# Moving the coefficient and artanh chains of layer 1 from VectorE to GpSimd in a four-layer graph network

## The chip, the cores and the metric

The kernel runs on one core of a Trainium2 chip. Its time is the device time of the core in microseconds, the median of several runs; lower is better. The engines are TensorE (PE), VectorE (DVE), ScalarE (ACT), GpSimd (POOL) and SyncE (SP), each with its own queue of instructions that it works through in order. Every DMA is issued from SyncE.

## The reference

128 graphs of 64 nodes with 128 features, and a sparse weighted adjacency matrix per graph, pass four layers. Each layer is a residual: `x = x + layer(relu(layernorm(x)), adj)`. The change touches layer 1, a graph network in hyperbolic space, and the small bias of layer 0 in front of it. Cut to what matters here (c = 1):

```python
y = ssp(y @ Wd1.T + bd1) @ Wd2.T + bd2          # end of layer 0
...
h = proj(mobius_add(proj(mobius_matvec(W, x)), hyp_bias))        # "nodes"
x_loc = logmap(h_i, h_j)                                          # for all pairs
a = silu(concat(x_self, x_loc) @ att_w1.T + att_b1)               # "edges"
adj_att = sigmoid(a @ att_w2.T + att_b2)
support = sum_j(adj_att * x_loc * mask)
u = silu(concat(x_self, support) @ mlp_w1.T + mlp_b1) @ mlp_w2.T + mlp_b2 + x_self
second = tanh(0.5 * lambda_x(h) * norm(u)) * u / norm(u)
out = proj(mobius_add(h, second))                                 # "rest1"
xt = silu(artanh(norm(out)) * out / norm(out))
out = proj(tanh(norm(xt)) * xt / norm(xt))
```

`mobius_add(x, y)` is `(ca * x + cc * y)`, with the coefficients `ca = (1 + 2xy + y2) / den`, `cc = (1 - x2) / den`, `den = 1 + 2xy + x2*y2` of three scalar products per node. All this is per node: one number per row of 128 features, so four numbers per partition in the layout below.

## The kernel before

**Tiling.** Eight graphs form a group: four pairs of graphs, a pair on the 128 partitions (64 nodes each). There are 16 groups. A tile of node features is 128x4x128 (128x512), a tile of pairs of nodes 128x4x64 (128x256), and a number per node is a 128x4 tile. Edges are packed into slots (512 columns for most, 264 for the last block), so edge tiles have 1024 or 528 columns.

**Stages of a group.** load; order (nodes sorted by degree; its side stream normed_x makes sr, a and xp, the last two with 128x512 products on GpSimd); layer0 (a filter per edge); layer1_nodes (end of layer 0, h, then the coefficients pq, qn and Sx of the edges); layer1_edges (attention scores, ex and th on ScalarE); rest1 (the sum over the neighbours, u, the Mobius addition, artanh, silu); rest2 (layers 2 and 3). The stages of neighbouring groups overlap: while edges and rest1 of groups g and g-1 run, order, layer0 and nodes of later groups do too.

**What sets the order.** Each stage is a Python generator that says, by `yield on(engine, ...)`, on which engine its next piece runs. A planner (class Weave) picks the pieces one by one: earliest possible start by its own costs, then a key that is the stage's rank plus a number from the table LATE for each piece. So the order of each engine's queue is fixed when the program is built, and every engine keeps it even where a piece turns out late. The planner counts four engines, their latencies and the rings of buffers. Its costs on GpSimd, for n columns, are one line:

```python
    return (0.5 + 0.14 * n) if ALU.pow in args else 0.18 + 0.0024 * n
```

**ScalarE's tables.** exp and ln need one table, silu and tanh another. The main loop runs the pieces in stretches of one table, and leaves a stretch only when named events have come: the silu stretch ends when the edges of a group and the silu part of rest1 (`rest1_silu`) of the group before are issued.

**The parts that change.** `layer1_nodes` begins by adding the bias bd1 to a PSUM tile on DVE. At its end it splits pq into three bf16 parts (pqs) and Sx into three (S3), all differences on DVE. `rest1` computes u, its norm un2 (ScalarE, sums of squares), then `un` by a power on GpSimd; `rb`, `ur`, `k_` and the coefficients d_ca, d_cc (function `mobius`) on DVE with four columns each; ScalarE scales hh by d_ca, DVE adds cc times u; ScalarE sums the squares again (d_n2), GpSimd takes the root (d_hn), DVE runs `artanh_over` to get the factor d_r, and ScalarE applies silu with the scale d_r. After that comes one more norm (un, ur, k_) and x2.

GpSimd has a power function: `power(dst, src, e)` is a tensor_tensor with ALU.pow against a constant tile, so it also serves as reciprocal and square root.

Of the kernel before, what the change touches and what calls it, by code (L numbers as in the profile page):

```python
# [29 lines left out]
MAXNORM = 1.0 - 0.004  # L30
# [741 lines left out]
PE, DVE, ACT, POOL = "PE", "DVE", "ACT", "POOL"  # L772
# [12 lines left out]
def about(engine, op, args, kw):  # L785
# [14 lines left out]
    if engine == ACT:  # L800
# [5 lines left out]


LATE = {
    "attention": (0, -0.5),
    "coefs_of": (1.25, 0.75, -2.25),  # L810
    "coefs_of2": (2.75,),
    "duo": (2.5, 3.5),
    "duo2": (0, 2.5, -2),
    "filter_of": (0.75, 3, -0.25, -2.25, -2, -2.75),
    "filter_of2": (-2.75, 1.75, 2.5, 1.75, -2.5),
    "layer1_nodes": (0, -0.25, 0, 0, 0, 0, 0, 3, -3.5, 0, 0, 0, -0.5, -5.5, 0, 2.25, -1.75, 0, 0, 0,
        0, 0, 0, -2.5, 0, 0, 0, 0, 0, -1.25, 0, 0, 0, 2, 0, 0.75, 0, 0, 0, 0, 0, 0, 0, 0, 0.5),
    "neighbours": (-0.25, -3.5),
    "neighbours2": (1.25,),
    "normed_x": (0, 0, 0, 0, 0, 0, 1.5),  # L820
    "one_minus_z": (3.75,),
    "order": (-0.25, -2.75, 2.25, 0, 0, -5, 0, -3.75, 0, 1.75, -6.75, -3, 3.5, 0, 0, -2.75, -2.75,
        3.25, 1.75, 0.5),
    "rest1": (-3, 0, 0, -3, 0, 0, 0, -3.5, -1.75, 0, 0, 0, 0, 0, -1.75, 0, 0, 0, 3.75),
    "rest2": (2.25, 4.5, 0, 0, 0, 0, 0, 0, 0, 0, 0, -4, 0, -3.75, 0, 1.25, 0, 0, 0, 0, -3, 0, -2.25,
        0, -3.5, 0, 0, 1.25, 3),
    "rows": (0, -1.25),
    "rows2": (2.5,),
    "scores_of": (-1.25, -1.5, -3.5, -1.5),
    "scores_of2": (0, -3.25, 0, -3.5),  # L830
    "slots_ranks": (3.5, 0, 4.75),
    "squares": (2.25, 9.5),
    "squares2": (0, 2.75),
    "turned_from": (3.5,),
    "weights_of": (-3,),
    "weights_of2": (0, -2.5, -2.25),
}


# [30 lines left out]
def on(engine, *takes, after=(), table=None):  # L870

    return engine, takes, after, table
# [98 lines left out]
def sparse_stack(ctx: ExitStack, tc: tile.TileContext, ins, out: bass.AP, flag):  # L971
# [7 lines left out]
    dense = ctx.enter_context(tc.tile_pool(name="s_dense", bufs=1))  # L979
# [106 lines left out]
    b1, bd1, b2s = (column("L0_gnn_" + n) for n in ("b1", "bd1", "b2"))  # L1086
# [49 lines left out]
    hby2 = const.tile([P, 1], F32, name="hby2")  # L1136
# [101 lines left out]
    act = S.activation  # L1238
# [43 lines left out]
    def power(dst, src, e):  # L1282

        G.tensor_tensor(dst, src, exps[e][:, 0:elements(src)], ALU.pow)
# [38 lines left out]
        act(dst, src, AF.Ln)  # L1323
        act(dst, dst, AF.Exp, scale=e)

    def artanh_over(r, s, hn):


        E, ef, num, den, q = (ttile(f"ah{k}") for k in range(5))
# [6 lines left out]
        V.scalar_tensor_tensor(num, E, 1.0, s, ALU.add, ALU.mult)  # L1336
        V.tensor_scalar(q, E, -1.0, 1.0, ALU.mult, ALU.add)
        V.tensor_tensor(num, num, q, ALU.add)
        V.tensor_tensor(den, q, s, ALU.mult)
        V.scalar_tensor_tensor(den, den, 1.0, E, ALU.add, ALU.add)  # L1340
        V.reciprocal(den, den)
        V.tensor_tensor(num, num, den, ALU.mult)
        V.tensor_tensor(den, num, num, ALU.mult)
        V.tensor_scalar(q, den, 1.0 / 9, None, ALU.mult)
        for c in (1.0 / 7, 1.0 / 5, 1.0 / 3):
            V.scalar_tensor_tensor(q, q, c, den, ALU.add, ALU.mult)
        V.scalar_tensor_tensor(q, q, 1.0, num, ALU.add, ALU.mult)
        V.tensor_tensor(q, q, ef, ALU.add)
        V.reciprocal(den, hn)
        V.tensor_tensor(r, q, den, ALU.mult)  # L1350

    def part(t, at, k, n):

# [284 lines left out]
        w.event("layer0", g)  # L1638


    def mobius(ca, cc, xx, xy, y2):

        den = ttile("den")
        V.tensor_scalar(ca, xy, 2.0, 1.0, ALU.mult, ALU.add)
        V.tensor_tensor(den, xx, y2, ALU.mult)
        V.tensor_tensor(den, den, ca, ALU.add)
        V.tensor_tensor(ca, ca, y2, ALU.add)
        V.tensor_scalar(den, den, 1e-15, None, ALU.max)
        V.reciprocal(den, den)
        V.tensor_tensor(ca, ca, den, ALU.mult)  # L1650
        V.tensor_scalar(cc, xx, -1.0, 1.0, ALU.mult, ALU.add)
        V.tensor_tensor(cc, cc, den, ALU.mult)

    def layer1_nodes(g, st):

# [3 lines left out]
        spn, ex = wtile("a0"), wtile("a1")  # L1659
        pt = bank()  # L1660
        pre = flat(pt)
# [73 lines left out]
        s, r = ttile("s"), ttile("r")  # L1735
# [6 lines left out]
        z, rs, mask = ttile("at_z"), ttile("at_r"), ttile("at_k")  # L1742
# [34 lines left out]
        mobius(ca, cc, xx, xy, hby2.to_broadcast([P, NP]))  # L1777
        V.tensor_tensor(ca, ca, t, ALU.mult)
        yield on(ACT)
        for p in range(NP):  # L1780
# [3 lines left out]
        hn, sc = ttile("hn"), ttile("sc")  # L1784
# [110 lines left out]
        cs = ttile("cs", bufs=2)  # L1895
        reduce_d(cs, dc)

        yield on(DVE, after=[("U", g)])
        pqs = dense.tile([P, 3, NP, N], BF, name="pqs", tag="pqs")
        V.tensor_copy(pqs[:, 0], pq)  # L1900
        V.tensor_tensor(e4, pq, pqs[:, 0], ALU.subtract)
        V.tensor_copy(pqs[:, 1], e4)
        V.tensor_tensor(pqs[:, 2], e4, pqs[:, 1], ALU.subtract)
# [99 lines left out]
    def rest1(g, st):  # L2003
# [53 lines left out]
        def product_with_h():  # L2057
            yield on(POOL)
            G.tensor_tensor(tmp2, u, hh, ALU.mult)
            yield on(DVE)  # L2060
            reduce_d(uh, tmp2)
            V.tensor_scalar(rb, st["beta"], 1e-15, None, ALU.max)
            V.reciprocal(rb, rb)
# [16 lines left out]
        V.tensor_tensor(xy, uh, k_, ALU.mult)  # L2080
        V.tensor_tensor(un2, un2, k_, ALU.mult)
        V.tensor_tensor(un2, un2, k_, ALU.mult)
# [9 lines left out]
        squares_sum(hn2, tmp, u)  # L2092
        yield on(POOL)
        G.tensor_scalar(hn2, hn2, MIN_NORM2, None, ALU.max)
        power(hn, hn2, 0.5)
# [7 lines left out]
        squares_sum(un2, tmp, u)  # L2103
        yield on(POOL)
        G.tensor_scalar(un, un2, MIN_NORM2, None, ALU.max)
        power(un, un, 0.5)
# [4 lines left out]
        V.reciprocal(ur, un)  # L2111
# [191 lines left out]
```

## Time and profile before

| | |
|---|---|
| time, median of 3 runs | 2124.41 us (2123.33 to 2126.65) |
| the profiled execution: its time, its span | 2121.52 us, 2119.6 us |
| granted TensorE clock, mean | 0.94 |
| VectorE, TensorE, ScalarE, GpSimd busy | 1847.9, 1806.3, 1641.1, 364.5 us |
| instructions on VectorE, ScalarE, GpSimd | 4828, 3364, 362 |
| DMA | 13.94 MB, 7 GB/s on the mean |

The span is the time from the first to the last instruction. A busy time is the union of an engine's instructions, without register, branch, semaphore and DMA-issuing ones. Nearly all instructions are recorded by one helper (line 853), so that groups have to be told apart by the tiles they write and read (`out<-in`), not by line. In a group's row stand the count, the total busy time and the mean of one; in a tile's row the smallest, middle and largest duration in ns. In the timeline the columns are start, duration, engine, operation, tiles and shapes.

Between the start (about 240 us) and the tail (from about 1860 us) the program repeats group by group. There VectorE is busy 1516.0 of 1620 us and TensorE 1450.6; in the tail, where less is left to overlap, VectorE is busy 161.8 of 259.6 us.

### The profile page before, as it was taken

The page shows a single profiled execution, that of the slowest core. Times are in us where ns is not written, and L with a number is a line of the kernel's source. Part 1 is how long each engine was busy: PE and PEld are TensorE (multiplying, and loading weights), DVE is VectorE, ACT ScalarE, POOL GpSimd, SP SyncE. Part 2 cuts the span into 40 slices and gives each one's busy share as a digit, 9 for nine tenths or more (in the row PEclk, how much of TensorE's full clock was granted, in tenths as well). Part 3 has the DMA queues.
Part 4 walks back from the last instruction along what each step waited for, and adds up shares of the span by engine and source line. Part 5 has one row for each costly group of instructions (what it writes and reads, how often), then busy time and mean ns, then how long its engine had stood idle before and what let it go on. Part 6 is the DMA issues. An engine that isn't in the chain of part 4 may idle for free.

```text
span 2119.6 us, 31941 instructions
## 1 busy us (share of the span) xinstructions
PE 1806.3 (85%) x11223; PEld 866.0 (41%) x11223; DVE 1847.9 (87%) x4828; ACT 1641.1 (77%) x3364; POOL 364.5 (17%) x362
## 2 busy tenths in 40 slices
PE   4869897998989898998989889898989889896773
PEld 2333343444444344444444444444434444443342
DVE  5669789999999999999999999999999999897742
ACT  3767887979698887979798897969888796975531
POOL 1011012021212203021221202121220302111121
PEclk9979999999999999999999999999999999997765
DMA  2000000000000000000000000000000000000000
GB/s 55 3 6 1 1 6 1 6 8 6 1 8 6 8 6 8 6 8 6 1 8 6 9 6 9 6 1 8 6 9 1 9 1 6 1 1 6 6 5 8
DMA packets 29531, 13.94 MB, mean 7 GB/s; under 512 B 10544, under 2 KB 29360, under 8 KB 29360
## 3 DMA queue, kind: packets, MB, share of 16 engines
q1 hardware_dynamic: 29360, 11.80, 2.1%
q8 instruction: 90, 1.47, 0.3%
q14 instruction: 81, 0.66, 0.1%
HBM read 7.61 MB, written 4.19 MB: 6 GB/s over the span
## 4 chain that ended last, share of the span: by engine, by line
PE 37%; DVE 36%; ACT 19%; issue 7%; POOL 0%; SPq 0%; DMA 0%; DVEq 0%; ACTq 0%; POOLq 0%
PE big L853 25%; PE sm L853 9%; ACT ex L853 6%; DVE va L853 5%; DVE ex L853 4%; PE sl L853 4%; ACT e L853 4%; DVE th L853 4%; DVE y L853 2%; ACT ra L853 2%; DVE ah L853 2%; DVE v L853 2%; ACT n L853 2%; DVE att L853 2%; DVE oh L853 1%
## 5 line engine op out<-in xcount | busy, mean ns | idle before, releaser
L853 PE MATMUL big<-ex,w2T 128*128 128x512 f32 (+1 forms) x768 | 320.2, 542 | 41.8 <-ACT ex L853 20.6
L853 ACT ACTIVATE ex<-big,c_L_gnn_att_b 128x1024 f32<-128x1024 f32 (+1 forms) x192 | 185.5, 974 | 105.0 <-PE big L853 103.2
L853 PE MATMUL big<-e,w1T 64*128 64x512 f32 (+1 forms) x768 | 201.5, 624 | 68.0 <-ACT e L853 47.8
L853 ACT ACTIVATE ex<-big,c_L_gnn_b 128x1024 f32<-128x1024 f32 (+1 forms) x192 | 185.7, 976 | 44.1 <-PE big L853 44.0
L853 PEld LDWEIGHTS big<-ex,w2T 128*128 128x128 f32 x768 | 131.7, 189 | 198.6 <-ACT ex L853 69.5
L853 PE MATMUL big<-va,U 64*128 64x512 f32 (+1 forms) x768 | 186.5, 563 | 29.1 <-DVE va L853 26.8
L853 PE MATMUL big<-va,a 64*128 64x512 f32 (+1 forms) x768 | 181.1, 568 | 10.7 <-DVE k_s L853 3.8
L853 PE MATMUL sl<-ex,aw2b 128*64 128x512 f32 (+1 forms) x768 | 180.7, 549 | 5.5 <-ACT th L853 4.3
L853 DVE SCALAR_TENSOR_TENSOR ex<-big,c_L_gnn_b,ra 128x1024 f32<-128x1024 f32 x128 | 163.7, 1279 | 16.0 <-PE big L853 15.6
L853 ACT ACTIVATE ex<-ex 128x1024 f32<-128x1024 f32 (+1 forms) x192 | 173.9, 925 | 0.2
L853 ACT ACTIVATE ra<-big 128x528 f32<-128x528 f32 (+1 forms) x192 | 166.3, 886 | 8.1 <-PE big L853 7.6
L853 DVE TENSOR_REDUCE y<-ex 128x128 f32<-128x1024 f32 x128 | 155.3, 1213 | 0.6
L853 ACT ACTIVATE th<-sl,hab 128x512 f32<-128x512 f32 (+1 forms) x192 | 118.1, 615 | 45.4 <-PE sl L853 45.4
L853 PE MATMUL big<-slot_r,Sx 64*128 64x512 bf16 (+1 forms) x1152 | 138.9, 346 | 0.0
L853 POOL TENSOR_TENSOR k_r<-k_r,exp 128x4 f32<-128x4 f32 x32 | 32.4, 1013 | 583.1 <-DVE k_r L853 578.7
L853 PEld LDWEIGHTS big<-e,w1T 64*128 64x128 f32 x768 | 68.9, 204 | 155.6 <-ACT e L853 55.1
L853 ACT ACTIVATE va<-va,sr 128x512 f32<-128x512 f32 (+1 forms) x192 | 123.1, 650 | 3.1 <-DVE va L853 2.9
L853 PE MATMUL big<-oh,pqs 64*64 64x512 bf16 (+1 forms) x1152 | 123.3, 348 | 0.0
L853 DVE COPY_PREDICATED va<-slot_r,big 128x1024 f32<-128x1024 uint16 (+1 forms) x96 | 106.5, 1111 | 9.7 <-PE big L853 9.7
L853 DVE SCALAR_TENSOR_TENSOR th<-th,oh 128x1024 f32<-128x1024 f32 (+1 forms) x80 | 99.2, 1240 | 13.8 <-ACT th L853 13.8
L853 ACT ACTIVATE e<-e 128x1024 f32<-128x1024 f32 (+2 forms) x144 | 106.7, 752 | 1.1
L853 PE MATMUL big<-va,ones 64*64 64x512 f32 (+1 forms) x768 | 97.4, 559 | 11.0 <-DVE va L853 11.0
(479 smaller groups left out, 3832.4 us busy)
## 6 DMA issues: line engine op xcount, KB each, us to landing
x<-in_x_dram SPq DMA_DIRECT2D x16, 256.0 KB, 2.9
out_dram<-v SPq DMA_DIRECT2D x16, 256.0 KB, 2.3
adj<-in_adj_dram SPq DMA_DIRECT2D x16, 128.0 KB, 2.3
rt<-in_L_gnn_att_w_dram SPq DMA_DIRECT2D x2, 64.0 KB, 1.9
rs<-in_L_gnn_mlp_w_dram SPq DMA_DIRECT2D x2, 64.0 KB, 2.0
wupd<-in_L_gnn_W_upd_dram SPq DMA_DIRECT2D x1, 128.0 KB, 3.6
w<-in_L_gnn_W_msg_dram SPq DMA_DIRECT2D x2, 64.0 KB, 3.3
r_L_gnn_bd<-in_L_gnn_bd_dram SPq DMA_DIRECT2D x1, 64.0 KB, 3.1
```

What stands on the lines that cost most here:

```text
L853: return f(*args, **kw)
```

## The change

Six edits and a new order:

1. bd1 is added by ScalarE (Identity with a bias) instead of DVE.
2. The first two bf16 parts of pq are made by ScalarE; the two differences stay on DVE.
3. The two differences of the split of Sx move from DVE to GpSimd, between ScalarE's two copies.
4. In rest1 everything from `rb` to `cc * k_` moves from DVE to GpSimd, reciprocals as powers with exponent -1; `mobius` takes the engine as an argument (the call in layer1_nodes keeps DVE).
5. `artanh_over` becomes `artanh_parts` (five operations on DVE) and `artanh_of` (18 operations and a power on GpSimd), with the division by the norm as a power of -0.5 and a product after it. The bound of s moves to GpSimd.
6. `ur` is a power of -0.5 on GpSimd, placed in front of the power that makes `un`, in both norms.

The table LATE has other numbers throughout, which changes the order of the pieces on every engine.

```diff
 LATE = {
-    "attention": (0, -0.5),
-    "coefs_of": (1.25, 0.75, -2.25),
...
+    "attention": (0, 0, 3.5, 1),
+    "duo": (4.5, 6.5),
...
-    for e in (0.5, -0.5, -0.25):
+    for e in (0.5, -0.5, -0.25, -1.0):
...
+    def artanh_of(r, E, ef, s):
+
+        num, den, q, z = (ttile(f"ah{k}") for k in range(2, 6))
+        G.tensor_scalar(num, E, 1.0, None, ALU.add)
+        G.tensor_tensor(num, num, s, ALU.mult)
+        G.tensor_scalar(q, E, -1.0, 1.0, ALU.mult, ALU.add)
+        G.tensor_tensor(num, num, q, ALU.add)
+        G.tensor_tensor(den, q, s, ALU.mult)
+        G.tensor_scalar(z, E, 1.0, None, ALU.add)
+        G.tensor_tensor(den, den, z, ALU.add)
+        power(den, den, -1.0)
+        G.tensor_tensor(num, num, den, ALU.mult)
+        G.tensor_tensor(z, num, num, ALU.mult)
+        G.tensor_scalar(q, z, 1.0 / 9, 1.0 / 7, ALU.mult, ALU.add)
+        for c in (1.0 / 5, 1.0 / 3, 1.0):
+            G.tensor_tensor(q, q, z, ALU.mult)
+            G.tensor_scalar(q, q, c, None, ALU.add)
+        G.tensor_tensor(q, q, num, ALU.mult)
+        G.tensor_tensor(r, q, ef, ALU.add)
...
-    def mobius(ca, cc, xx, xy, y2):
+    def mobius(E, ca, cc, xx, xy, y2):
...
-        V.reciprocal(den, den)
...
+        (power(den, den, -1.0) if E is G else V.reciprocal(den, den))
...
-        yield on(DVE)
-        V.tensor_scalar(flat(spn), pre, bd1, None, ALU.add)
-        w.release("sm")
+        yield on(ACT)
+        act(flat(spn), pre, AF.Identity, bias=bd1)
+        w.release("sm")
+        yield on(DVE)
...
+        for k in range(2):
+            yield on(ACT)
+            act(pqs[:, k], (pq, e4)[k], AF.Copy)
+            yield on(DVE)
+            V.tensor_tensor((e4, pqs[:, 2])[k], (pq, e4)[k], pqs[:, k], ALU.subtract)
...
-            yield on(DVE)
-            V.tensor_tensor(Sx if k == 0 else S3[2], Sx, S3[k], ALU.subtract)
+            yield on(POOL)
+            G.tensor_tensor(Sx if k == 0 else S3[2], Sx, S3[k], ALU.subtract)
...
         yield on(POOL)
+        G.tensor_scalar(rb, st["beta"], 1e-15, None, ALU.max)
+        power(rb, rb, -1.0)
         G.tensor_scalar(un, un2, MIN_NORM2, None, ALU.max)
+        power(ur, un, -0.5)
         power(un, un, 0.5)
-        yield on(DVE, after=[("uh", g)])
-        V.tensor_tensor(rb, rb, un, ALU.mult)
-        V.reciprocal(ur, un)
+        G.tensor_tensor(rb, rb, un, ALU.mult)
         yield on(ACT, table="silu")
         act(k_, rb, AF.Tanh)
-        yield on(DVE)
-        V.tensor_tensor(k_, k_, ur, ALU.mult)
+        yield on(POOL, after=[("uh", g)])
+        G.tensor_tensor(k_, k_, ur, ALU.mult)
         xy, ca, cc = ttile("d_xy"), ttile("d_ca"), ttile("d_cc")
...
-        mobius(ca, cc, h2, xy, un2)
-        V.tensor_tensor(cc, cc, k_, ALU.mult)
+        mobius(G, ca, cc, h2, xy, un2)
+        G.tensor_tensor(cc, cc, k_, ALU.mult)
...
         power(hn, hn2, 0.5)
-        yield on(DVE)
-        V.tensor_scalar(s, hn, MAXNORM, None, ALU.min)
-        artanh_over(r, s, hn)
+        G.tensor_scalar(s, hn, MAXNORM, None, ALU.min)
+        yield on(DVE)
+        artanh_parts(E, ef, s)
+        yield on(POOL)
+        artanh_of(r, E, ef, s)
+        power(hn2, hn2, -0.5)
+        G.tensor_tensor(r, r, hn2, ALU.mult)
```

More of the change, by code (lines that the diff above doesn't have):

```diff
@@ L808 @@
 LATE = {
-    "attention": (0, -0.5),
-    "coefs_of": (1.25, 0.75, -2.25),
[L811 to L819, printed above, removed]
@@ L820 @@
-    "normed_x": (0, 0, 0, 0, 0, 0, 1.5),
-    "one_minus_z": (3.75,),
[L822 to L834, printed above, removed]
+    "attention": (0, 0, 3.5, 1),
+    "duo": (4.5, 6.5),
+    "duo2": (1.25,),
+    "filter_of": (1.5, 3.5, -1.75, 0, 0, -1.5),
+    "filter_of2": (-2.5, 1.5, 2.5, 4),
+    "layer1_edges": (0, 0, 0, -4),
+    "layer1_nodes": (0, 0, 0, 0, 0, -3.5, 0, 0, -2.75, 0, 0, 3, 2.25, 0, 3.5, 3.75, 0, -3.5, 0, 0,
+        0, 0, 3, 0, 0, 0, 0, 0, 0, 0, 0, 2.25, 2.5, 2.5, 0, 0, 0, 2.75, 0, 0, 0, 0, 0, 0, 0, 1.5, 0,
+        0, 0, -3.25),
@@ new lines @@
+    "neighbours": (0, -2.25),
+    "neighbours2": (0, 2.25),
+    "norm_of_h": (4.25,),
+    "normed_x": (2.75,),
+    "one_minus_z": (3.75,),
+    "order": (0, 0, 0, 1.5, 0, -2.75, 0, 0, 0, 5.5, -1.5, 0, 0, 0, 0, 2.5, 0, 0, 2, -4),
+    "product_with_bias": (0, 3.25),
+    "rest1": (-3, 0, -3.25, -3.25, 0, 0, 0, -3.5, 0, -3.25, 0, 0, 0, 0, 0, 1.75, 0, -1.5),
+    "rest2": (0.25, 0, 0, -3.5, 0, 0, 0, 0, 1.25, 0, 0, 0, 0, 0, 0, 1.75, 0, 0, -2.25, 0, -3, 0, 0,
+        0, 0.75, -1.75, -4, 0, 2.25),
@@ L835 @@
+    "rows": (-1, -3.5),
+    "rows2": (1.75,),
+    "scores_of": (-1.25, 0, -2.5),
+    "scores_of2": (0, 0, 0, -5),
+    "slots_ranks": (2.25,),
+    "squares": (2.25, 7.5),
+    "turned_from": (0, 4),
     "weights_of": (-3,),
-    "weights_of2": (0, -2.5, -2.25),
+    "weights_of2": (0, 0, -0.75),
 }
@@ L1324, in root, with artanh_parts @@
         act(dst, dst, AF.Exp, scale=e)
-    def artanh_over(r, s, hn):
-        E, ef, num, den, q = (ttile(f"ah{k}") for k in range(5))
+    def artanh_parts(E, ef, s):
         V.tensor_scalar(E, s, -ROOT_HALF, ROOT_HALF, ALU.mult, ALU.add)
@@ L1335, in artanh_over @@
                         ALU.add, ALU.mult)
[L1336 to L1340, printed above, removed]
-        V.reciprocal(den, den)
[L1342 to L1350, printed above, removed]
+    def artanh_of(r, E, ef, s):
[16 more added lines that the diff above has]
+        G.tensor_tensor(r, q, ef, ALU.add)
     def part(t, at, k, n):
@@ L1638, in layer0 @@
         w.event("layer0", g)
-    def mobius(ca, cc, xx, xy, y2):
[L1643 to L1652, printed above, removed]
+    def mobius(E, ca, cc, xx, xy, y2):
+        den = ttile("den" if E is V else "g_den")
+        E.tensor_scalar(ca, xy, 2.0, 1.0, ALU.mult, ALU.add)
+        E.tensor_tensor(den, xx, y2, ALU.mult)
+        E.tensor_tensor(den, den, ca, ALU.add)
+        E.tensor_tensor(ca, ca, y2, ALU.add)
+        E.tensor_scalar(den, den, 1e-15, None, ALU.max)
+        (power(den, den, -1.0) if E is G else V.reciprocal(den, den))
+        E.tensor_tensor(ca, ca, den, ALU.mult)
+        E.tensor_scalar(cc, xx, -1.0, 1.0, ALU.mult, ALU.add)
+        E.tensor_tensor(cc, cc, den, ALU.mult)
     def layer1_nodes(g, st):
@@ L1776, in layer1_nodes @@
         V.tensor_tensor(xx, xx, t, ALU.mult)
-        mobius(ca, cc, xx, xy, hby2.to_broadcast([P, NP]))
+        mobius(V, ca, cc, xx, xy, hby2.to_broadcast([P, NP]))
         V.tensor_tensor(ca, ca, t, ALU.mult)
@@ L1896, in layer1_nodes @@
         reduce_d(cs, dc)
-        yield on(DVE, after=[("U", g)])
[L1899 to L1903, printed above, removed]
-        yield on(DVE)
+        pqs = dense.tile([P, 3, NP, N], BF, name="pqs", tag="pqs")
+        for k in range(2):
[3 more added lines that the diff above has]
+            V.tensor_tensor((e4, pqs[:, 2])[k], (pq, e4)[k], pqs[:, k], ALU.subtract)
+        yield on(DVE, after=[("U", g)])
         Sx, S3 = st["Sx"], [wide.tile([P, NP, P], BF, name=f"Sx{k}", tag=f"Sx{k}") for k in range(3)]
@@ L2061, in product_with_h @@
             reduce_d(uh, tmp2)
-            V.tensor_scalar(rb, st["beta"], 1e-15, None, ALU.max)
-            V.reciprocal(rb, rb)
             w.event("uh", g)
@@ L2069, in rest1 @@
         yield on(POOL)
+        G.tensor_scalar(rb, st["beta"], 1e-15, None, ALU.max)
+        power(rb, rb, -1.0)
         G.tensor_scalar(un, un2, MIN_NORM2, None, ALU.max)
+        power(ur, un, -0.5)
         power(un, un, 0.5)
-        yield on(DVE, after=[("uh", g)])
-        V.tensor_tensor(rb, rb, un, ALU.mult)
-        V.reciprocal(ur, un)
+        G.tensor_tensor(rb, rb, un, ALU.mult)
         yield on(ACT, table="silu")
         act(k_, rb, AF.Tanh)
-        yield on(DVE)
-        V.tensor_tensor(k_, k_, ur, ALU.mult)
+        yield on(POOL, after=[("uh", g)])
+        G.tensor_tensor(k_, k_, ur, ALU.mult)
         xy, ca, cc = ttile("d_xy"), ttile("d_ca"), ttile("d_cc")
-        V.tensor_tensor(xy, uh, k_, ALU.mult)
-        V.tensor_tensor(un2, un2, k_, ALU.mult)
-        V.tensor_tensor(un2, un2, k_, ALU.mult)
-        mobius(ca, cc, h2, xy, un2)
-        V.tensor_tensor(cc, cc, k_, ALU.mult)
+        G.tensor_tensor(xy, uh, k_, ALU.mult)
+        G.tensor_tensor(un2, un2, k_, ALU.mult)
+        G.tensor_tensor(un2, un2, k_, ALU.mult)
+        mobius(G, ca, cc, h2, xy, un2)
+        G.tensor_tensor(cc, cc, k_, ALU.mult)
         yield on(ACT)
@@ L2094, in rest1 @@
         G.tensor_scalar(hn2, hn2, MIN_NORM2, None, ALU.max)
+        E, ef = ttile("ah0"), ttile("ah1")
         power(hn, hn2, 0.5)
+        G.tensor_scalar(s, hn, MAXNORM, None, ALU.min)
         yield on(DVE)
-        V.tensor_scalar(s, hn, MAXNORM, None, ALU.min)
-        artanh_over(r, s, hn)
+        artanh_parts(E, ef, s)
[3 more added lines that the diff above has]
+        G.tensor_tensor(r, r, hn2, ALU.mult)
         yield on(ACT, table="silu")
@@ L2105, in rest1 @@
         G.tensor_scalar(un, un2, MIN_NORM2, None, ALU.max)
+        power(ur, un, -0.5)
         power(un, un, 0.5)
@@ L2110, in rest1 @@
         yield on(DVE, "x2")
-        V.reciprocal(ur, un)
         V.tensor_scalar(k_, k_, MAXNORM, None, ALU.min)
```

## The prediction

> **What bounds the kernel now.** First the page's busy times: VectorE (DVE) leads, TensorE (PE) is next, GpSimd (POOL) is nearly free.
>
> ```profile
> PE 1806.3 (85%) x11223; PEld 866.0 (41%) x11223; DVE 1847.9 (87%) x4828; ACT 1641.1 (77%) x3364; POOL 364.5 (17%) x362
> ```
>
> The chain's shares say that no engine holds the end alone.
>
> ```profile
> PE 37%; DVE 36%; ACT 19%; issue 7%; POOL 0%; SPq 0%; DMA 0%; DVEq 0%; ACTq 0%; POOLq 0%
> ```
>
> In its middle the program repeats every 121 us, once per group. ScalarE (ACT) splits a period by its table loads; the timeline gives the edges (two more loads, inside the silu stretch, serve the softplus).
>
> ```profile
> 1148.18 1.28 ACT L853 ACT_TABLE_LOAD   x1
> 1206.83 1.28 ACT L853 ACT_TABLE_LOAD   x1
> 1269.02 1.28 ACT L853 ACT_TABLE_LOAD   x1
> ```
>
> So 58.65 us with silu tables, 62.2 us with log tables, 120.8 together. Busy time in the two:
>
> ```profile
> core 0: us, PE busy (x) PEld busy (x) DVE busy (x) ACT busy (x) POOL busy (x), PEclk, DMA share, GB/s
> 1148.20:1206.80 58.60, 54.12 (x372) 25.80 (x371) 56.92 (x131) 43.93 (x101) 15.10 (x14) 1.00 0.03 8
> 1206.80:1269.40 62.60, 54.66 (x330) 26.19 (x331) 57.60 (x169) 58.67 (x111) 7.81 (x8) 0.97 0.02 5
> ```
>
> In the silu stretch DVE is busy 97%, PE 92%, ACT 75%; in the log stretch ACT leads with 94%. DVE work is worth time in the first only, ACT work is dear in the second.
>
> The silu stretch carries rest1, one long dependent chain: u, the coefficients k_, d_ca, d_cc, the update of w, its norm, the artanh chain to d_r, then ACT's silu with d_r. In the timeline u is ready at 1155.15 and ACT begins with d_r at 1184.09: **28.9 us**.
>
> **What the Trainium skill says.** "SBUF — State Buffer", section "Who interferes with whom": DVE and GpSimd share one port pair under an exclusive lock. A DVE instruction with two SBUF inputs and a GpSimd instruction that reads SBUF exclude each other; one with a single SBUF input does not contend. The trace agrees:
>
> ```profile
> 1038.81 2.52 POOL L853 TENSOR_TENSOR a<-xp,o_mv 128x512 f32<-128x512 f32 x1
> 1040.35 1.00 DVE L853 TENSOR_TENSOR rb<-rb,un 128x4 f32<-128x4 f32 x1
> 1041.37 2.25 DVE L853 TENSOR_TENSOR oh<-pos,slot_k 128x2048 bf16<-128x2048 bf16 x1
> 1041.42 3.33 POOL L853 TENSOR_TENSOR xp<-xp,r_L_gnn_bd 128x512 f32<-128x512 f32 x1
> 1043.54 1.22 DVE L853 TENSOR_TENSOR k__9670<-k__9670,ur 128x4 f32<-128x4 f32 x1
> ```
>
> The xp product alone takes 1.27 us; here it waits out the 2.25 us oh instruction, and then the four-column k_ product waits 1.06 us for it. Four-column GpSimd operations get stuck too:
>
> ```profile
> L853 POOL TENSOR_SCALAR un<-un x32: 227/232/1160, 307.1 to 2072.1; 128x4 f32<-128x4 f32 x32
> L853 POOL TENSOR_TENSOR d_hn<-d_n,exp x16: 1037/1312/4315, 320.6 to 2064.5; 128x4 f32<-128x4 f32 x16
> ```
>
> The 4.3 us one sat behind th (1.21) and oh (2.28) in a row. In the other direction they cost DVE nothing visible: beside a power at 1074.3 four x updates ran in 1.14 us, as elsewhere. "GPSIMD Engine Reference", section "Elementwise — side-by-side cycle accounting", has GpSimd's tensor_tensor at 1.96 times DVE's; here 128x512 take 1.27 against 0.68 us, 1.9 times.
>
> **The change part by part**, per group. The order of instructions shows what each engine issues: DVE loses 656, 41 a group; GpSimd gains 43; ACT 3; PE, SyncE, DMAs and table loads keep their numbers.
>
> - *DVE.* Artanh 16 instructions 2.61 us (0.15 to 0.18 each) and the s bound 0.16; rb 1.13 (three), ur 0.33 (two), k_ by ur 1.22; xy, un2 twice and cc by k_ 0.64; mobius 9 for 1.48; bd1 0.74; two casts 0.58; two Sx differences 1.37. Sum 10.3 us. Of this 1.9 (0.84 at rb, 1.06 at k_) is waiting for a and xp, which stay and will hold other two-input instructions. Real relief: **8.4 us**, 6.5 in the silu stretch, 1.9 in the log stretch.
> - *ACT.* bd1 as an Identity from PSUM, 0.60 (nearest row: a<-sm, 596 ns), and two 128x256 copies, about 0.41 each: +1.4 us. The order also moves ACT work. At start-to-start steps of dense stretches (1.00 us for 1024 columns, 0.60 for 528, 0.56 for 512, 0.36 for 256, 0.32 for 128) the log stretch holds 58.6 us before and 62.2 after, the silu stretch 38.5 and 36.2. Where 58.6 took 62.2 us, 62.2 take **66.0**.
> - *GpSimd.* 35 four-column operations, start to start 0.31 (1156.66 to 1156.97); 6 powers, 1.1; two 128x512 differences, 1.27: 10.9 + 6.6 + 2.5 = 20 us on top of 22.9. No throughput limit. The two differences may hold DVE up to 1.27 us each; beside the one-input reductions and PSUM reads of the log stretch I take half, and offset it with that stretch's DVE relief. Sx has about 15 us of DVE work until the scores need it, so its slower chain costs nothing.
>
> **The rest1 path** decides. From u, on free ports: u by hh to 1.4; rb pair to 2.8; un, two powers (the new ur one stands first) and rb by un to 5.6; tanh 5.95; ten small operations and a power, ca at 10.1; cc at 11.0; w update 12.1. On GpSimd sr, its power, a and xp now stand between d_cc and d_n: 3.9 us, to 14.9. d_n, power, s to 16.6; five DVE instructions to 17.6; 18 small and one power to 24.3; last power and product: d_r at **25.7**, better than 28.9.
>
> With the lock it is later. Followed with DVE's new order beside it (va spreads 1.2 us, th 1.2, oh pieces 0.3 to 0.4, v+x 0.7: two SBUF inputs each), one GpSimd operation passes per such DVE instruction instead of three or four. cc comes at 15 to 16, so DVE, whose own work before the w update lasts 10.5, waits 4 to 5 us. sr, a and xp push d_n to 20 or 21; artanh takes 9 or 10 instead of 8.1: d_r at 31.5 to 34. The bounds are 25.7 and 34; I take **30.5**: nearer the contended end, because instructions with two SBUF inputs fill half of DVE's silu stretch today (29 of 58.6 us, added up from the timeline), and below it, because a waiting DVE frees the port.
>
> While d_r is late, ACT stands before the silu with d_r; behind it in ACT's queue are softplus, the th and ex of the scores, hence PE's PSUM banks. That is the new wait.
>
> Period: log 66.0; silu load to u 4.6 (load 1.3, v copy and hid 1.2, PE 1.3, u 0.7, where before v's four pieces and a ra stood there too); u to d_r 30.5; after d_r 19.4 us of ACT steps, between 20.6 (pace of the log stretch) and 23.5 (pace of today's 18.8 in 22.7), middle 22.0. Sum 123.1 against 120.8: +2.3. Times 14 full periods: +32. In the tail there is no cover: the last rest1 pays artanh (d_r 3.7 us after s today; with 1.0 + 6.7 + 1.4, 9.1) and one power, together 6.5; other bare stretches and group 0 add 2.5. **Total +41 us.**
>
> The profiled execution took 2121.5 (span 2119.6 plus 1.9), 2.9 below the median 2124.4, inside the runs' 3.3 us spread; I put the sum on the median: **2165 us**. About 0.2% (4 us) is what a measurement of this kernel tells from no change.
>
> **Rivals.**
> - *The relief arrives* (faster, 0.27). d_r at 25.7 and ACT at log pace afterwards: 66.0 + 4.6 + 25.7 + 20.6 = 116.9, -3.9 times 14 is -55, tail +9: about 2079. For it: DVE at 97% and rest1's pieces on the chain of waits; with fewer DVE instructions the port is freer. It decides at d_r 28.2 us after u, where the period is today's. Against it: the locks shown, and a planner whose costs know no lock.
> - *PE sets the pace, nothing moves* (0.05). PE's 108.8 us per period are untouched; a little relief only pays for the tail: 2124.
> - *Full contention* (within slower): d_r at 34, 23.5 after it: 128.1, +7.3 times 14, tail 14: about 2240.
> - That the change doesn't do what it says is excluded by the instruction order.
>
> **How the numbers follow.** Slower 0.68, faster 0.27, same 0.05. The range 2082 to 2230 leaves out about a tenth on each side, the ends of d_r early and late. The slower case alone: 2135 to 2235.
>
> **What would show it.** DVE busy falls to about 1700 to 1730 with its idle time grown, mainly before w updates; ACT waits for POOL at d_ca and d_r by 2 us or more a group; small GpSimd medians stretch well over 232 ns; silu stretch near 57, log near 66. I am wrong if ACT's wait for d_r stays under 1 us a group, or if the log stretch stays at 62.

## The result: 163 us slower, and where a group's time went

The changed kernel takes 2287.12 us (median of 4 runs, 2282.97 to 2288.81) against 2123.87 us of the kernel before: ratio 1.0767, 95% interval 1.0745 to 1.079. The direction was forecast; the size was put at 41 us, a quarter of what came, and 2287 lies above the forecast range of 2082 to 2230. The profiled execution took 2287.22 us (span 2285.4). First the page, busy times and chain shares:

```profile
PE 1856.3 (81%) x11223; PEld 880.0 (39%) x11223; DVE 1730.3 (76%) x4172; ACT 1662.8 (73%) x3412; POOL 676.2 (30%) x1051
PE 34%; DVE 26%; ACT 23%; POOL 11%; issue 5%; DMA 0%; SPq 0%; DVEq 0%; ACTq 0%; POOLq 0%
```

VectorE lost 118 us of work, as intended, and the busiest engine is now TensorE with 81% of the span. GpSimd, absent from the chain before, holds 11% of it. The timeline's table loads again cut out one period:

```profile
1368.17 1.28 ACT L853 ACT_TABLE_LOAD   x1
1430.82 1.28 ACT L853 ACT_TABLE_LOAD   x1
1499.70 1.28 ACT L853 ACT_TABLE_LOAD   x1
```

Silu stretch 62.65 us, log stretch 68.9, together 131.5 (121 before). Cut further, at u and at the silu with d_r, busy times by stretch (columns as before: length, then each engine's busy time):

```profile
core 0: us, PE busy (x) PEld busy (x) DVE busy (x) ACT busy (x) POOL busy (x), PEclk, DMA share, GB/s
1368.20:1374.80 6.60, 5.00 (x23) 2.30 (x23) 6.32 (x8) 2.54 (x4) 0.00 (x0) 1.00 0.01 2
1374.80:1405.10 30.30, 26.89 (x164) 11.39 (x160) 21.72 (x46) 16.37 (x39) 25.85 (x49) 1.00 0.05 14
1405.10:1430.80 25.70, 19.97 (x174) 10.14 (x172) 18.78 (x41) 22.65 (x55) 9.27 (x10) 1.00 0.00 1
1430.80:1499.70 68.90, 58.28 (x344) 28.03 (x345) 59.89 (x164) 61.92 (x117) 8.43 (x6) 0.98 0.02 5
```

These four lengths are the terms of the prediction's sum. The table gives them for every run as means over the same seven middle groups, from the start times in each timeline: silu load to the end of the u addition; from there to ScalarE's start with d_r (in brackets: d_r ready); from there to the log load; the log stretch.

| kernel | load to u | u to d_r | d_r to log load | log | period |
|---|---|---|---|---|---|
| before | 7.0 | 28.9 (28.8) | 22.7 | 62.5 | 121.2 |
| **forecast** | 4.6 | 30.5 | 22.0 | 66.0 | 123.1 |
| **changed** | 6.6 | 30.5 (30.1) | 25.8 | 69.0 | 131.9 |
| e1 new order, old engines | 7.7 | 31.6 (25.4) | 28.5 | 68.6 | 136.4 |
| e2 old order, new engines | 7.0 | 39.2 (39.1) | 24.1 | 63.0 | 133.2 |
| e5 old order, coefficients moved | 7.0 | 33.1 (32.8) | 23.4 | 62.5 | 126.0 |
| e6 old order, artanh moved | 7.0 | 34.1 (34.1) | 22.9 | 62.4 | 126.3 |
| e7 old order, bd1, pqs, Sx moved | 7.0 | 29.1 (28.8) | 22.9 | 62.8 | 121.8 |
| e15 as e2, rb early, ur last | 7.0 | 35.9 (35.9) | 23.2 | 62.6 | 128.7 |
| e9 new order, coefficients back | 6.6 | 32.8 (31.2) | 25.8 | 68.9 | 134.2 |
| e10 new order, artanh back | 6.6 | 35.1 (24.1) | 25.7 | 68.9 | 136.4 |
| e11 new order, bd1, pqs, Sx back | 7.7 | 29.5 (29.4) | 27.4 | 68.6 | 133.1 |
| e12 new order, rb early, ur last | 6.6 | 28.8 (28.8) | 25.7 | 68.6 | 129.7 |

(A period is averaged by itself, so it can differ by 0.1 from the sum of its row.) The term that the prediction argued at length, u to d_r, came out at the number it took. The others failed.

### The profile page after: what moved, and what is told of

The parts are those of the page before. It is cut to its first block, busy times and chain, and to the rows that moved or that the text cites. A ratio compares the mean times of both kernels' runs of the same rounds, so it can differ in the third digit from the quotient of the medians.

```text
span 2285.4 us, 32190 instructions
## 1 busy us (share of the span) xinstructions
PE 1856.3 (81%) x11223; PEld 880.0 (39%) x11223; DVE 1730.3 (76%) x4172; ACT 1662.8 (73%) x3412; POOL 676.2 (30%) x1051
## 4 chain that ended last, share of the span: by engine, by line
PE 34%; DVE 26%; ACT 23%; POOL 11%; issue 5%; DMA 0%; SPq 0%; DVEq 0%; ACTq 0%; POOLq 0%
PE big L853 21%; PE sm L853 10%; ACT ex L853 5%; DVE va L853 4%; ACT e L853 3%; PE sl L853 3%; DVE th L853 3%; ACT ra L853 3%; ACT n L853 2%; POOL rb L853 2%; ACT L853 2%; DVE ex L853 2%; DVE att L853 2%; POOL un L853 2%; ACT w L853 1%
## 5 line engine op out<-in xcount | busy, mean ns | idle before, releaser
L853 PE MATMUL big<-ex,w2T 128*128 128x512 f32 (+1 forms) x768 | 333.9, 560 | 36.3 <-ACT ex L853 21.5
L853 PE MATMUL big<-va,U 64*128 64x512 f32 (+1 forms) x768 | 192.3, 578 | 51.1 <-DVE va L853 48.2
L853 POOL TENSOR_TENSOR k_r<-k_r,exp 128x4 f32<-128x4 f32 x32 | 45.7, 1429 | 627.9 <-DVE k_r L853 584.9
L853 PE MATMUL sl<-ex,aw2b 128*64 128x512 f32 (+1 forms) x768 | 185.7, 562 | 38.2 <-ACT th L853 28.8
L853 PE MATMUL big<-va,a 64*128 64x512 f32 (+1 forms) x768 | 194.0, 588 | 13.6 <-ACT ex L853 5.8
L853 ACT ACTIVATE ra<-big 128x1024 f32<-128x1024 f32 (+1 forms) x192 | 168.1, 887 | 39.5 <-PE big L853 36.9
L853 DVE SCALAR_TENSOR_TENSOR th<-th,oh 128x1024 f32<-128x1024 f32 (+1 forms) x80 | 105.2, 1315 | 39.3 <-ACT th L853 39.1
L853 DVE TENSOR_TENSOR va<-oh,adjT 128x1024 f32<-128x1024 bf16 (+6 forms) x160 | 119.8, 792 | 7.9 <-PE big L853 6.3
L853 POOL TENSOR_TENSOR n<-n,Sx 128x512 f32<-128x512 f32 x16 | 18.6, 1160 | 355.9 <-ACT Sx L853 355.9
```

The source lines that it names most:

```text
L853: return f(*args, **kw)
```

## Experiments

All but e3 and e4 keep one of the two orders piece by piece. The planner is charged with what that order was planned for (`plan`), and only the engine that issues an operation is changed; in e5, e8, e12, e15, e17 and e18 a few GpSimd operations also stand at another place, named there. `rawV`, `rawG` and `rawA` are the three engines without the planner's charge, and `ng_power` is `power` on `rawG`. In what follows the brackets behind a time are the 95% interval of its ratio to the kernel before, which took 2121.8 to 2122.7 us beside these runs. Cut:

```diff
+    def plan(engine, op, *args, **kw):
+
+        w.ran(engine, about(engine, op, args, kw))
...
-        V.tensor_scalar(flat(spn), pre, bd1, None, ALU.add)
+        plan(DVE, "tensor_scalar", flat(spn), pre)
+        rawA.activation(flat(spn), pre, AF.Identity, bias=bd1)
```

So TensorE's and SyncE's queues stay the same, instruction by instruction, and the other engines' queues lose or gain only the operations that are moved. What is put back on VectorE under the new order stands where its piece was planned for GpSimd, not at a place sought for VectorE.

### Order against engines

e1 takes the changed kernel and issues every moved operation on its old engine; e2 takes the kernel before and issues every one on its new engine; e3 and e4 are the two kernels with an empty table:

```diff
-LATE = {
-    "attention": (0, -0.5),
...
+LATE = {}
```

> The new order of pieces, kept piece by piece, with every moved operation issued again on the engine that had it before (coefficient and artanh chains, ur, bd1, the bf16 copies and the Sx differences). Theory 'engines' (the GpSimd chains and the waits they bring cost the 163 us): near the kernel before, 2110 to 2150 us. Theory 'order' (the new positions in the queues cost them whatever engine runs the pieces): near the changed kernel, 2270 to 2300 us. If both share: in between.

> The order of before, kept piece by piece, with every moved operation issued on its new engine. Theory 'engines': 2270 to 2300 us, about 10 us more per group, with ScalarE or VectorE waiting for GpSimd at d_ca, d_cc and d_r. Theory 'order': 2110 to 2165 us, the upper end being what the prediction's own sum for the engines alone gives.

> The kernel before with the table LATE empty, so the planner's own order. It measures what an order found by the table is worth here. Theory 'order': the order is worth 100 us or more, so this takes 2220 to 2330 us. Theory 'engines': the order is worth little, 2125 to 2180 us.

> The changed kernel with the table LATE empty. Theory 'order' (the new table is a bad one for the chip): no slower than the changed kernel, 2230 to 2300 us. Theory 'engines': 150 us or so above the kernel before with an empty table.

| | old engines | new engines |
|---|---|---|
| old order | 2124 | e2: 2285.97 (1.0717 to 1.0784) |
| new order | e1: 2333.94 (1.0969 to 1.1011) | 2287 (1.0745 to 1.079) |
| empty table | e3: 2406.95 (1.1313 to 1.1352) | e4: 2410.93 (1.134 to 1.1379) |

Neither theory holds alone: e2 came where 'engines' put it, e1 and e3 came out slower than either theory had them, and e4 between its two. Moving the chains under the old order costs 164 us, the new order under the old engines costs 212, and both together cost 163: they overlap, they do not add. The new order recovers nothing against the old one with the new engines; under the new order itself the moves gain 47 us (e1 less the changed kernel). With an empty table the engines make no measurable difference. The found order was worth 285 us to the old engines (2407 less 2122) and is worth 124 to the new ones (2411 less 2287).

What e2 loses is seen in one period. Four answers of its timeline: VectorE, GpSimd, then ScalarE, VectorE (in brackets the idle time before an instruction and what ended it):

```profile
1371.74 4.65 DVE L853 TENSOR_TENSOR oh<-pos,slot_k 128x2048 bf16<-128x2048 bf16 x3
```

```profile
1371.81 5.45 POOL L1370 TENSOR_TENSOR un<-un,exp 128x4 f32<-128x4 f32 x1
```

```profile
1406.64 1.28 ACT L853 ACTIVATE w<-w,d_r 128x128 f32<-128x128 f32 x4 [6.07 <-POOL d_r L2192]
```

```profile
1409.70 0.43 DVE L853 TENSOR_SCALAR a<-a 128x512 f32<-128x512 f32 x1 [8.72 <-ACT a L1743]
```

The power for un, 1.01 us alone, waits out three oh instructions at the lock and takes 5.45. The product rb with un then stands behind sr, a and xp in GpSimd's queue, and the tanh comes 13.7 us after u instead of 8.0. The artanh chain begins 5.1 us later than before, and from its first operation to d_r it takes 9.0 us where VectorE alone took 3.7. So d_r comes 10.3 us later, ScalarE stands in front of it for 6.07 us, and bd1, next in ScalarE's queue, holds VectorE for 8.72 and, through the PSUM bank that it empties, TensorE for 4.76. This is the wait that the prediction described, in the order for which it was not computed. The Trainium skill says in "PSUM — Partial Sum Buffer", section "Engine vs sequencer instructions", that the queues of ScalarE, VectorE and GpSimd are strict FIFO; these lines agree: the matmul for bd1 was over at 1403.25, and bd1 ran at 1408.99, behind d_r's instructions.

The TensorE clock is a rival here. The traces show it granted at 1.00 or, in the middle of the program for 3.4 or 6.8 us at a time (at times longer in e3 and e4), at 0.50. Over the same seven groups its mean is 0.98 in the kernel before and 0.97 in the changed one, so it is not what separates these two: the difference is about 1 us of the 10.7 a period. In e2 it is 0.92, and TensorE is busy 59.21 us in a silu stretch, for the 372 products that took 54.12 us in the kernel before:

```profile
1360.50:1430.90 70.40, 59.21 (x372) 28.39 (x371) 50.32 (x95) 44.48 (x104) 30.97 (x55) 0.90 0.02 7
```

How much of e2's 12.0 us a period is the clock's was not separated. An estimate from the timelines is up to 3 us: between the update of w and the artanh chain VectorE loses 1.6 us, 1.11 of them in one wait for TensorE, and behind d_r the stretch is 1.4 us longer.

### The parts under the old order

e5 moves only the coefficient chain (with rb times un right behind un), e6 only artanh, e7 only bd1, the pq copies and the Sx differences. e15 is e2 with three places changed on GpSimd:

```diff
         def x_self():
             yield on(POOL)
+            rawG.tensor_scalar(rb, st["beta"], 1e-15, None, ALU.max)
+            ng_power(rb, rb, -1.0)
...
-        rawG.tensor_scalar(rb, st["beta"], 1e-15, None, ALU.max)
-        ng_power(rb, rb, -1.0)
...
+        ng_power(un_r, un, 0.5)
+        rawG.tensor_tensor(rb, rb, un_r, ALU.mult)
         ng_power(ur, un, -0.5)
-        ng_power(un, un, 0.5)
...
-        rawG.tensor_tensor(rb, rb, un, ALU.mult)
```

> The order of before; only the coefficient chain of rest1 (rb to cc, with ur) runs on GpSimd, and rb times un stands right behind un in GpSimd's queue instead of behind sr, a and xp. Theory 'late d_r' (what the moved chain adds to the way from u to d_r comes out as time, once a group): un waits out DVE's oh instructions at the lock and k_ stands behind a and xp, so d_r is about 6 us late, 15 times: 2200 to 2230 us. Theory 'only both together are too slow' (each part alone fits into the slack): 2115 to 2140 us.

> The order of before; only the artanh chain (and the division by the norm) runs on GpSimd, the first five operations stay on DVE. Theory 'late d_r': 5.3 us more from d_n to d_r as in the run with all parts, less the 0.7 us that DVE work leaves: 2180 to 2205 us. Theory 'only both together': 2115 to 2140 us.

> The order of before; only bd1 and the two bf16 copies of pq run on ScalarE and the two Sx differences on GpSimd; rest1 is as before. Theory 'late d_r': nothing here lies on the way to d_r, and the log stretch kept its length in the run with all parts: 2115 to 2135 us. Theory 'ScalarE is full in the log stretch' (it leads with 94%, so 0.8 us of copies a group and two slower GpSimd differences come out): 2135 to 2160 us.

> The order of before with every moved operation on its new engine, as in the earlier run with all parts, but on GpSimd the reciprocal of beta is taken at the start of rest1, rb times un stands right behind un (ahead of sr, a and xp), and ur behind both. Theory 'queue and lock' (most of what the coefficient chain added was place in the queue): u to d_r falls from 39 to 32 to 34 us, 2180 to 2215 us. Theory 'the engine' (GpSimd's own durations): 37 us or more, 2250 to 2280 us.

e5 took 2180.9 us (1.0253 to 1.0298), e6 2204.66 (1.0364 to 1.0423), e7 2128.98 (1.0024 to 1.0046), e15 2237.76 (1.0516 to 1.0556). In the table the log stretch and the load to u stay within 0.5 us of before in all of them; the way from u to d_r grows by 4.2, 5.2, 0.2 and 7.0 us, the period by 4.8, 5.1, 0.6 and 7.5. So under the old order a late d_r comes out about one for one, and each chain costs by itself: there was no slack. (In e6 no stretch of half clock falls between u and d_r, so there the clock is no rival.) e5 and e15 missed their figures, e5 on the cheap side, e15 between its two theories. In e15 the tanh came as early as in the kernel before (8.0 us after u), but the lock met the next instruction in GpSimd's queue, the root for sr, and k_ stood behind it:

```profile
1341.93 5.36 POOL L853 TENSOR_TENSOR sr<-sr,exp 128x4 f32<-128x4 f32 x1
1347.27 1.59 POOL L853 TENSOR_TENSOR a<-xp,o_mv 128x512 f32<-128x512 f32 x1
1348.93 1.28 POOL L853 TENSOR_TENSOR xp<-xp,r_L_gnn_bd 128x512 f32<-128x512 f32 x1
1350.18 0.42 POOL L2163 TENSOR_TENSOR k__12177<-k__12177,ur 128x4 f32<-128x4 f32 x1
```

### The parts under the new order

e9, e10 and e11 put the same three parts back on VectorE in the changed kernel; e12 is the changed kernel with the places of e15.

> The changed kernel and its order, piece by piece; only the coefficient chain of rest1 is issued on VectorE again. Theory 'positions' (ScalarE reaches the silu with d_r at 30.5 us whether d_r is early or late; the rest is where the pieces stand): 2270 to 2300 us. Theory 'the chain is still in it' (VectorE's 3.7 us of waiting for d_cc goes on through its queue to va, TensorE and the scores): 2225 to 2260 us.

> The changed kernel and its order; only artanh is issued on VectorE again, at the place of its first five operations. Theory 'positions': d_r is ready about 5 us earlier and ScalarE can't use it, 2275 to 2300 us. Theory 'the chain is still in it': the 83 us that the artanh chain cost in the order of before come back, 2200 to 2230 us.

> The changed kernel and its order; bd1, the two bf16 copies and the Sx differences are back on VectorE. Theory 'positions': 2270 to 2300 us. Theory 'VectorE waits for bd1 on ScalarE' (3.8 us of waiting at the bound of bd1 in nearly every group): 2235 to 2260 us.

> The changed kernel and its order; on GpSimd the reciprocal of beta is taken at the start of rest1 and ur behind un and rb, so tanh, d_ca and d_cc come 2 to 4 us earlier. Theory 'positions': 2270 to 2290 us. Theory 'the chain is still in it': 2 to 3 us a group, 2240 to 2260 us.

e9 took 2311.71 us (1.0876 to 1.0915), e10 2327.76 (1.0958 to 1.0995), e11 2300.34 (1.0811 to 1.0859), e12 2259.88 (1.0639 to 1.0683): everything put back made the new order slower, by 25, 41 and 13 us. All three lie above both of their theories, e11 by less than 1 us. e10 had d_r ready 24.1 us after u, 6 us earlier than the changed kernel, and ScalarE came to it 4.6 us later. Its timeline, ScalarE, shows where:

```profile
1423.68 1.11 ACT L853 ACTIVATE ex<-big,c_L_gnn_att_b 128x1024 f32<-128x1024 f32 x1 [6.61 <-PE big L853]
```

That score ex stands in front of the silu with d_r and waits 6.61 us for TensorE (2.46 in the changed kernel). TensorE needs va, and VectorE copies va only after the 22 operations from the bound of s to d_r that now stand in front, where the changed kernel has five: 24.0 us after u instead of 21.4. The rest comes with a lower TensorE clock. The next lines are the product of va in the changed kernel, the same in e10, and the stretch of half clock in which e10's falls:

```profile
1397.52 1.13 PE L853 MATMUL big<-va,U 64*128 64x512 f32 x4 [1.27 <-DVE va L853]
1420.29 2.08 PE L853 MATMUL big<-va,U 64*128 64x512 f32 x4 [3.84 <-DVE va L853]
1418.50:1425.10 6.60, 4.81 (x14) 1.80 (x16) 3.99 (x7) 1.11 (x1) 0.00 (x0) 0.50 0.00 0
```

No run holds the clock fixed, so the share of each is read from the timeline and not tested; e9 has such stretches before d_r too. e12 came in the range of "the chain is still in it": tanh 2.1 us and d_r 1.3 us earlier, the period 2.2 shorter, 27 us gained. Across the changed kernel, e9, e10 and e12 the load to u stays at 6.6 us, the end of the silu stretch at 25.7 to 25.8, the log stretch at 68.6 to 69.0: these three belong to the order, not to the engines. (e1 and e11, with bd1 and the Sx differences back, move the first two by 1 to 3 us and not the log stretch.)

### Does ScalarE's content set the log stretch?

e13 repeats each bf16 copy of Sx three more times in the kernel before; e14 and e16 give the two copies to GpSimd in the kernel before and in the changed one.

```diff
             act(S3[k], Sx, AF.Copy)
+            for _ in range(3):
+                nc.scalar.activation(S3[k], Sx, AF.Copy)
```

> The kernel before; in the log stretch each of the two bf16 copies of Sx is made four times by ScalarE instead of once (6 more of about 0.52 us, 3.1 us a group, as much as the new order moved into that stretch). Theory 'content' (the log stretch is as long as ScalarE's work in it): 15 times 3.1 us, 2160 to 2175 us, log stretch 65.5. Theory 'waits' (ScalarE's 3.9 us of idle time in the stretch take it up): 2122 to 2140 us.

> The kernel before; the two bf16 copies of Sx are made by GpSimd instead of ScalarE, 1.04 us less on ScalarE in the log stretch. Theory 'content': up to 1 us a group, 2105 to 2117 us. Theory 'waits': 2119 to 2126 us. Rival 'Sx late' (the chain of four 128x512 operations takes 2 to 4 us more and the lock holds it up): 2130 to 2150 us.

> The changed kernel and its order; the two bf16 copies of Sx are made by GpSimd instead of ScalarE, 1.04 us less on ScalarE in the log stretch. Theory 'content': 0.7 to 1 us a group, 2270 to 2278 us. Theory 'waits': 2283 to 2292 us, or slower where Sx comes late.

e13 took 2202.34 us (1.0351 to 1.0391). Busy times of its two stretches:

```profile
1323.20:1384.20 61.00, 55.81 (x372) 26.43 (x371) 58.00 (x132) 44.01 (x102) 15.33 (x14) 0.97 0.03 7
1384.20:1449.50 65.30, 55.25 (x330) 26.07 (x330) 56.78 (x168) 61.98 (x116) 7.75 (x8) 0.95 0.02 5
```

ScalarE is busy 61.98 us in the log stretch, 3.3 more than the 58.67 that the prediction shows, and the log stretch grew from 62.5 to 65.5: most of the added work came out, as "content" said. The silu stretch grew by another 2.3 us, which puts the time above both theories. TensorE had a clock of 0.97 there instead of 1.00 and was busy 1.7 us longer for its 372 products; that this is the cause was not tested. Nor was it separated whether the log stretch pays for ScalarE's work or for the Sx chain, which the repeats make 3.5 us longer. The reverse does not hold: e14 took 2118.14 us (0.9977 to 0.9993), between its theories, with the log stretch at 62.8; e16 took 2292.76 (1.0782 to 1.0822), with 0.7 us less in the log stretch and 1.4 more in the silu stretch. Work added to this place comes out for the most part; work taken from it brings almost nothing.

### Reliefs together

e8 moves only what nobody waits for to GpSimd (the reciprocal of beta early, ur of the second norm behind un, the root of d_n2 to -0.5 beside VectorE's artanh); e17 adds the Sx copies of e14; e18 the Sx differences as well.

```diff
-        V.reciprocal(den, hn)
-        V.tensor_tensor(r, q, den, ALU.mult)
+        plan(DVE, "reciprocal", den)
+        V.tensor_tensor(r, q, hn, ALU.mult)
```

(here `hn` is given d_n2 to the power of -0.5, made by GpSimd.)

> The order of before; only operations that nobody waits for move to GpSimd: the reciprocal of beta at the start of rest1, ur of the second norm behind un, and the root of d_n2 to -0.5 beside DVE's artanh in place of the last reciprocal. DVE loses four instructions, about 0.7 us, in the silu stretch, the way to d_r one of 0.2 us. Theory 'late d_r': 0.2 to 1.0 us a group gained, 2105 to 2122 us. Rival 'GpSimd's queue' (the added powers hold up sr, a, xp and un): 2125 to 2145 us.

> The order of before; the off-path moves to GpSimd in rest1 (reciprocal of beta early, ur of the second norm, root of d_n2 beside artanh) together with the two bf16 copies of Sx on GpSimd: VectorE has 0.7 us less in the silu stretch, ScalarE 1.04 us less in the log stretch. Theory 'several engines end a stretch together': the stretches stay as long as TensorE and the other engine make them, 2112 to 2121 us. Theory 'each relief counts': 2095 to 2110 us.

> The same with the two Sx differences on GpSimd as well: in the log stretch ScalarE has 1.04 us and VectorE 1.37 us less. Theory 'several engines end a stretch together', with VectorE the second in the log stretch: 2100 to 2115 us. Theory 'the order holds the time' (or TensorE does): 2114 to 2124 us, as with one relief; rival 'Sx late' (four 128x512 operations in a row on GpSimd): 2125 to 2145 us.

e8 took 2121.96 us (ratio 0.9983 to 1.0008), e17 2121.25 (0.9987 to 1.0003), e18 2118.71 (0.9978 to 0.9994). In e8 d_r is ready 0.3 us earlier. In two periods of three ScalarE takes it 0.3 us earlier, and the period is still 120.8 or 121.4 us (120.8 or 121.5 before); in the third a stretch of half clock falls in front of it, ScalarE begins 0.7 us later than before, and the period is 123.1. In e18 the log stretch keeps 62.8 us with 1.04 us of ScalarE work and 1.37 of VectorE work gone. The best of these, e14 and e18, gain 0.15%; their intervals lie wholly below 1, but the gain is under the 0.2% that the prediction took as the least to be told from no change. All are far ahead of the changed kernel. Whether TensorE, its clock or the order itself holds the stretches of the kernel before is left open.

## The prediction, point by point

**Right, the first in part by luck: the way from u to d_r, and VectorE's busy time.** The 30.5 us taken are the 30.5 measured, between 25.7 and 34; VectorE's busy time fell to 1730.3 us. The waits at the coefficients came too, 2 us a group for d_ca and nearly 4 for d_cc; total us, times, longest:

```profile
DVE w L853 <- POOL d_cc L853: 49.3, 13, 6.7
...
ACT w L853 <- POOL d_ca L853: 29.9, 15, 3.7
```

The luck is in the parts of the way, which were off in both directions, and in its end, which was set by ScalarE's own arrival and not by a wait for d_r. Tanh came at 8.0 us where 5.95 stood for free ports, since the product with hh, rb's maximum and rb times un waited at the lock (2.19, 1.20 and 0.75 us; in e2, where these three stood free, 1.28, 0.23 and 0.20). d_cc was used 13.9 us after u, not 15 to 16; d_n began at 18.5, not 20 to 21. GpSimd's timeline of the changed kernel:

```profile
1374.83 2.19 POOL L853 TENSOR_TENSOR w<-w,hh 128x512 f32<-128x512 f32 x1 [9.28 <-DVE w L853]
1377.10 1.20 POOL L853 TENSOR_SCALAR rb<-beta 128x4 f32<-128x4 f32 x1
1379.82 1.04 POOL L853 TENSOR_TENSOR ur<-un,exp 128x4 f32<-128x4 f32 x1
1383.08 1.16 POOL L853 TENSOR_TENSOR k__12158<-k__12158,ur 128x4 f32<-128x4 f32 x1 [0.32 <-ACT k__12158 L853]
1404.88 0.20 POOL L853 TENSOR_TENSOR d_r<-d_r,d_n 128x4 f32<-128x4 f32 x1
```

**Wrong: the small operations stretch.** Few do. Rows of one tile on GpSimd, smallest, middle and largest ns:

```profile
L853 POOL TENSOR_SCALAR ah<-ah x112: 191/221/1100, 331.6 to 2233.0; 128x4 f32<-128x4 f32 x112
L853 POOL TENSOR_TENSOR ah<-ah,ah x112: 198/199/1124, 332.3 to 2233.3; 128x4 f32<-128x4 f32 x112
```

The contended estimate let one GpSimd operation pass per two-input VectorE instruction. In the new order VectorE idles for 4.1 of the 8.9 us of the artanh chain in the period shown (0.38 and 3.76 us), and the middle values stay at the uncontended 0.2 us; where VectorE is dense, as at un in e2, not even one passes in three. (What the prediction takes from the section "Who interferes with whom" about instructions with one SBUF input is said there of those outside the 2-port perf modes only. The instructions that the prediction counts are two-input ones, reductions and PSUM reads.)

**Wrong: ScalarE waits for d_r.** By the prediction's own test (under 1 us a group) this failed. d_r is ready 30.1 us after u and ScalarE takes it at 30.5. The new order had moved ScalarE's arrival to the same moment; so the wait that was to carry the cost of the change was not there.

**The failed steps are the other three terms of the sum**, 8.8 us a period together. *Load to u*, 4.6 against 6.6: one TensorE step was left out. The two products with m1aT and m1bT take 2 us, and the first waited for the copy of v:

```profile
1370.10 1.13 PE L853 MATMUL sm<-w,m1aT 128*128 128x512 f32 x2 [0.82 <-ACT v L853]
1371.07 1.02 PE L853 MATMUL sm<-w,m1bT 128*128 128x512 f32 x2
```

*After d_r*, 22.0 against 25.8: ScalarE's busy time there is 22.65 us, 0.7 more than the 21.95 of the same stretch before (22.80 long):

```profile
1304.90:1327.70 22.80, 21.23 (x182) 10.93 (x180) 22.34 (x48) 21.95 (x54) 3.98 (x5) 1.00 0.07 18
```

So the content was forecast well (+0.6), but idle time grew from 0.9 to 3.1 us. *Log stretch*, 66.0 against 69.0: here too the content is right: ScalarE is busy 61.92 us, against 58.67 in the log stretch that the prediction shows, +3.3 where +3.6 was forecast, and e13 shows that such content is mostly paid. What was missed is idle time, 7.0 us against 3.9. ScalarE's waits in the log stretch, first the largest of the kernel before (two more have 0.3 us each), then those of the changed kernel (total us, times, longest):

```profile
ACT ex L853 <- PE big L853: 3.0, 4, 1.4
...
ACT ra L853 <- PE big L853: 2.6, 2, 1.4
ACT ex L853 <- PE big L853: 1.6, 1, 1.6
ACT nn L853 <- DVE nn L853: 1.4, 1, 1.4
ACT n L853 <- DVE ca L853: 0.7, 1, 0.7
```

The error behind the last two is one: content was multiplied by the pace of the old order, as if a new order kept the same few waits. That the waits belong to the order is shown by e9, e10 and e12, which keep these two lengths; which places in the order make them was not tested and stays open.

**Wrong: 14 equal periods.** From the silu load at 418.5 us (418.6 in the changed kernel) twelve periods follow. The first three take 140.8 us each in the changed kernel and 142.4 in e1, 121.9 before and 132.1 in e2, so they too belong to the order; the other nine take 131.6 against 121.3. Nine times 10.2, plus 56.5 for the first three, plus 17 at the end (9 forecast) is the 166 us between the two spans.

**The rivals.** *The relief arrives* failed: with 118 us less VectorE work the kernel is slower than before under either order, and where VectorE lost work and the way to d_r grew no longer (e8, e17, e18), at most 0.15% was gained. So VectorE's 97% of the silu stretch did not make its work worth time; that other engines end the stretch with it is likely and not shown. *PE sets the pace* (2124) and *full contention* (2240, d_r at 34) lie below the 2287 as well: both take the old pace for the other stretches.

**Sx at no cost** held within 7 us: e7, with bd1 and the pq copies in it as well, is 0.35% slower (0.24 to 0.46%).

## What to carry to other kernels

In a software pipeline whose queues are ordered in advance, a change has two prices, that of the operations and that of the new order, and they do not add: try the new engines under the old order, and the new order with the old engines, before explaining either. When an order is found anew, compare stretch by stretch what each queue holds and how long it idles; a content multiplied by the old pace misses the new waits. Here ScalarE work added at one place was mostly paid for, and ScalarE or VectorE work taken away under the old order gained almost nothing, so a high busy share alone does not promise a gain. Look at the granted clock of each stretch before a longer wait is put down to the edit.

## What the runs showed of the hardware

- A waiting GpSimd instruction can be passed by several VectorE instructions in a row: the four-column power took 5.45 us (1.01 alone) beside three two-input bf16 instructions of 4.65 us together, and everything behind it in GpSimd's queue waited too.
- Four-column operations on GpSimd take 0.19 to 0.23 us and start 0.28 to 0.31 us apart when the next needs the result; a four-column power takes 1.04 us. Artanh as 18 of them and a power lasted 8.1 us from its first GpSimd operation to d_r in e2, the last root and product included; all of VectorE's, the bound of s and the first five included, took 3.9 us in e10.
- Where the granted TensorE clock was 0.50, a group of four matmuls of one shape took 2.08 us (e10) instead of 1.13 (changed kernel, clock 1.00). Such stretches lasted 3.4 or 6.8 us in the middle of both kernels; what brings them on was not tested.
